# A four-layer Perceiver kernel: short steps of both passes together, queries at steps 4 to 6, the row constants at step 47, keys' and values' weights as two loads, and two more pieces in one feed-forward

## The chip, the cores and the metric

The kernel runs on one core of a Trainium2 chip, in one launch. The metric is the device time in microseconds (us). A core has five engines with instruction streams of their own: TensorE (PE, with PEld for its weight loads), VectorE (DVE), ScalarE (ACT), GpSimd (POOL) and SyncE (SP). SP and POOL issue nearly all transfers here, each in the order of its own queue; 16 DMA engines carry them.

## The reference

128 query rows x (128 x 256) pass through four layers. Each layer has a cross-attention over a context of 12,544 rows of 256, then an attention or mixing block on the 128 rows, then a feed-forward block. Everything is float32, with 16 heads of 16. The cross-attentions are what the change touches most:

```python
q = _split_heads(hidden_states @ q_w.T + q_b)
k = _split_heads(context @ k_w.T + k_b)
v = _split_heads(context @ v_w.T + v_b)
scores = jnp.einsum('bhqd,bhkd->bhqk', q, k) / jnp.sqrt(jnp.float32(HD))
scores = jnp.where(mask, -jnp.inf, scores)
probs = jax.nn.softmax(scores, axis=-1)
ctx = jnp.einsum('bhqk,bhkd->bhqd', probs, v)
```

Layer 1 adds a 128 x 12,544 table (`fside`) to the scores of every head, layers 0 and 3 mask some of the keys, and layers 1 to 3 project the result (`O @ Wo + bo`). The feed-forward of layer 1 is a mixture of 8 experts (`h = x @ w1 + b1`, layer norm, gelu, `@ w2 + b2`, the two best gates); that of layer 2 is a piecewise-linear gelu on numbers rounded to multiples of 2^-8, with 33 breakpoints.

## The kernel before

Twelve blocks run one after another: l0x, l0a, l0f, l1x, l1a, l1f, l2x, l2a, l2f, l3x, l3a, l3f (x: cross-attention, a: attention, f: feed-forward).

**Cross-attention (`cross`, from L419).** The 16 heads are taken as 4 units of 4 heads. The array of TensorE is used as four row tiles of 32, one for each head of a unit. The 12,544 keys are taken in 25 steps (`NST`) of 512 (`ST`); the last step of a unit has only 256 keys, and is called the short step here. Each unit passes over the keys twice:

- Pass 1, `score_s` (L498 on): scores with the queries on the partitions (matmul L515, tile `_s`). VectorE takes the maximum of each head's bank (L528; in l1x L523, which adds `fside` too). After a unit's last step `raised` puts the negative maximum into `low` (L538), and `lower` (L546, L547) adds it to the unit's queries, so that pass 2 yields scores less their maximum.
- Pass 2, `score_t` (L554 on): the scores transposed, keys on the partitions (L573, tile `_t`); ScalarE takes the exponential (L590, or L580 for two heads at once); in l1x VectorE adds the transposed `fside` first (L585). `values` multiplies by the values (L634, tile `_p`) and adds into `acc` (L640). `finish` transposes and divides (L645 to L650).

Pass 2 runs `lead` = 27 steps behind pass 1. Step `at` makes pass 1 of step `km = at` and pass 2 of step `ke = at - 27`, counted over all units from 0 to 99. So steps 0 to 26 hold pass 1 alone, steps 27 to 99 are mixed, steps 100 to 126 hold pass 2 alone. In a mixed step `scores` (L599) makes two sets: scores of heads 2, 3 beside transposed scores of heads 0, 1, and then the other way round. The matmuls of a set run on different row tiles at the same time. Short steps are number 24 of each unit: pass 1 takes them at 24, 49, 74 and 99, pass 2 at 51, 76, 101 and 126. In pass 2 alone, outside l1x, PSUM is taken as pairs of banks (`alone`, `pairs`), one exponential covers two heads, and `values` takes two steps at once.

**Order by hand.** The whole loop of `cross` stands under `manual_schedule`: each engine runs its instructions as the code issues them. So do the tail of l3x and all of l3a. In the other blocks a scheduler orders the instructions by their costs.

**Pieces.** Keys and values of all four layers are projected from the context by small jobs, the pieces, in one long list (`self.jobs`). A key piece is a projection of 128 columns for 512 keys (two matmuls 128x512, L373, tile `_k`); a value piece is one of 256 keys (four matmuls 128x256, tile `_v`). `pump(n)` runs the next n of them. In `cross` a goal and a `rate` say how many a step takes. In the other blocks `one`, which hands out a PSUM bank, adds `share` to a credit and pumps a piece for each whole one; l1f sets `share` to 0.9 (L1061). In l2f `pump(1)` stands behind every second breakpoint but the last (L1231).

A visit is 512 keys of one layer and one part ("k" or "v"). `load` (L185) fetches its context (tile `_c`) on SP's queue, three visits ahead. Results go to DRAM on POOL's queue (`kx` L220, `vx` L246) and come back on SP's: key tiles `kt` of 1,024 keys (`keys`, mask row L290 and four heads L294, 17 tiles held) and value tiles `vt` (`values`, L307, three tiles). `fetch_k(at + 2)` and `fetch_v` at the head of a step ask for what is used two steps later.

**Loads at the start.** SP's queue carries x, `l0x_kvw` (128 x 1024, the weights of keys and values, L194), the context of visit 0 (c0) and of visit 1 (c1), the columns of constants `cols` (L201), `cst` (L202), and visit 2. POOL's queue carries `w_l0x`, the weights of the queries (`ahead`, L323; `weight` asks for it). At step 2 of l0x POOL issues `rows`, a broadcast of 2,940 floats to 128 partitions (L663), and `ahead(2)` fetches the weights `w_l0a`; the next one, for l0f, follows.

**Queries.** `query(g)` (L450 on) makes the queries of unit g: two matmuls with the transposed normed x, and VectorE's scaling (L461). Unit 0 is made before the loop, units 1 to 3 at steps 12, 37 and 62.

## Time and profile before

Three runs took 2293.19, 2289.47 and 2293.31 us, median 2293.19. The profiled execution took 2290.23 us, its span is 2288.4 us, at a mean granted TensorE clock of 0.99. By stretches of the span (the blocks' bounds are rounded):

| stretch, us | blocks | PE busy | DVE busy | ACT busy | granted clock |
|---|---|---|---|---|---|
| 0 to 145 | l0x, steps 0 to 24 | 134.0 | 66.9 | 36.5 | 0.98 |
| 145 to 460 | l0x, the rest | 313.2 | 233.8 | 159.3 | 1.00 |
| 460 to 590 | l0a, l0f | 123.9 | 30.5 | 73.7 | 1.00 |
| 590 to 1210 | l1x | 615.9 | 514.9 | 322.1 | 0.99 |
| 1210 to 1405 | l1a, l1f | 193.5 | 98.8 | 97.4 | 1.00 |
| 1405 to 1760 | l2x | 349.4 | 266.4 | 214.5 | 1.00 |
| 1760 to 1835 | l2a, l2f | 69.3 | 45.1 | 36.5 | 0.98 |
| 1835 to 2190 | l3x | 347.5 | 266.7 | 211.1 | 1.00 |
| 2190 to 2288 | l3a, l3f | 86.0 | 27.1 | 25.4 | 0.93 |

The busy time of an engine is the time in which it had at least one instruction at work. PE counts as busy at half clock too, and also when only one of its row tiles has work. A clock of 1.00 is full speed. Groups and timelines name an instruction by its line, its output and its inputs, with how often it ran (x4) and the time; for TensorE the records count double, since a float32 matmul is recorded as two. Waits read "engine tile line <- what released it: total us, times, longest us".

### The profile page before, as it was taken

The page shows a single profiled execution, that of the slowest core. Times are in us where ns is not written, and L with a number is a line of the kernel's source. Part 1 is how long each engine was busy: PE and PEld are TensorE (multiplying, and loading weights), DVE is VectorE, ACT ScalarE, POOL GpSimd, SP SyncE. Part 2 cuts the span into 40 slices and gives each one's busy share as a digit, 9 for nine tenths or more (in the row PEclk, how much of TensorE's full clock was granted, in tenths as well). Part 3 has the DMA queues.
Part 4 walks back from the last instruction along what each step waited for, and adds up shares of the span by engine and source line. Part 5 has one row for each costly group of instructions (what it writes and reads, how often), then busy time and mean ns, then how long its engine had stood idle before and what let it go on. Part 6 is the DMA issues. An engine that isn't in the chain of part 4 may idle for free.

```text
span 2288.4 us, 76016 instructions
## 1 busy us (share of the span) xinstructions
PE 2232.8 (98%) x32141; PEld 1682.5 (74%) x32141; DVE 1550.2 (68%) x3391; ACT 1176.5 (51%) x2020; POOL 326.7 (14%) x587
## 2 busy tenths in 40 slices
PE   8999999999999999999999999999999999999979
PEld 3368888875647887666778854588888867888868
DVE  3476688713187789999987545988861699888231
ACT  2213366674323555555684364266677515666832
POOL 4331100002241110101001123200000440000001
PEclk9999999999999999999999999999999999999989
DMA  8886633228898887888766688633332863333217
GB/s 303 261 258 202 220 108 93 75 73 299 297 304 271 276 256 229 251 243 255 228 203 212 220 314 271 177 89 99 90 86 83 277 200 105 89 89 95 60 44 242
DMA packets 220977, 431.86 MB, mean 189 GB/s; under 512 B 31236, under 2 KB 87576, under 8 KB 216544
## 3 DMA queue, kind: packets, MB, share of 16 engines
q1 hardware_dynamic: 181440, 270.87, 40.7%
q0 software_dynamic: 38976, 156.03, 19.1%
q8 instruction: 256, 4.19, 0.8%
q14 instruction: 81, 0.66, 0.1%
q10 hardware_dynamic: 224, 0.10, 0.0%
HBM read 320.72 MB, written 106.16 MB: 187 GB/s over the span
## 4 chain that ended last, share of the span: by engine, by line
PE 54%; DVE 3%; ACT 2%; DMA 1%; issue 1%; POOL 1%; POOLq 0%; ACTq 0%; DVEq 0%
PE l3x_t L573 5%; PE l2x_t L573 5%; PE l2x_p L634 4%; PE l3x_p L634 4%; PE l2x_k L373 4%; PE l1x_t L573 4%; PE l3x_k L373 4%; PE l3x_s L515 3%; PE l1x_p L634 3%; PE l2x_s L515 3%; PE l2x_v L373 3%; PE l3x_v L373 2%; PE l1x_s L515 2%; PE l3f_h L373 1%; PE l3f_o L373 1%
## 5 line engine op out<-in xcount | busy, mean ns | idle before, releaser
L590 ACT ACTIVATE l1x_e<-l1x_e 128x512 f32<-128x512 f32 (+1 forms) x400 | 240.6, 622 | 209.1 <-DVE l1x_e L585 209.1
L528 DVE TENSOR_REDUCE l0x_mxs<-l0x_s 128x1 f32<-128x512 f32 (+1 forms) x400 | 244.3, 672 | 98.8 <-PE l0x_s L515 66.9
L523 DVE CUSTOM_DVE_ANT_0 l1x_j<-l1x_s,l1x_f 128x512 f32<-128x512 f32 (+1 forms) x400 | 252.9, 675 | 41.4 <-PE l1x_t L573 23.6
L528 DVE TENSOR_REDUCE l3x_mxs<-l3x_s 128x1 f32<-128x512 f32 (+1 forms) x400 | 242.4, 671 | 30.1 <-PE l3x_t L573 24.7
L528 DVE TENSOR_REDUCE l2x_mxs<-l2x_s 128x1 f32<-128x512 f32 (+1 forms) x400 | 242.3, 671 | 29.5 <-PE l2x_t L573 24.7
L585 DVE TENSOR_TENSOR l1x_e<-l1x_t,l1x_g 128x512 f32<-128x512 f32 (+1 forms) x400 | 250.0, 672 | 10.9 <-PE l1x_t L573 9.0
L590 ACT ACTIVATE l0x_e<-l0x_t 128x512 f32<-128x512 f32 x292 | 149.5, 596 | 167.4 <-PE l0x_t L573 164.4
L573 PE MATMUL l1x_t<-l1x_qb,kt 32*128 32x128 f32 x3136 | 203.0, 285 | 0.9 <-DVE l1x_e L585 0.7
L515 PE MATMUL l1x_s<-kt,l1x_qb 32*128 32x512 f32 (+1 forms) x800 | 196.2, 630 | 1.0 <-DMA kt<-l1x_kx 0.7
L590 ACT ACTIVATE l3x_e<-l3x_t 128x512 f32<-128x512 f32 x292 | 149.7, 595 | 82.0 <-PE l3x_t L573 78.9
L515 PE MATMUL l3x_s<-kt,l3x_qb 32*128 32x512 f32 (+1 forms) x800 | 188.2, 617 | 0.0
L590 ACT ACTIVATE l2x_e<-l2x_t 128x512 f32<-128x512 f32 x292 | 149.7, 595 | 74.7 <-PE l2x_t L573 71.6
L515 PE MATMUL l2x_s<-kt,l2x_qb 32*128 32x512 f32 (+1 forms) x800 | 187.2, 610 | 0.0
L515 PE MATMUL l0x_s<-kt,l0x_qb 32*128 32x512 f32 (+1 forms) x800 | 181.9, 614 | 2.0 <-DMA kt<-l0x_kx 2.0
L573 PE MATMUL l3x_t<-l3x_qb,kt 32*128 32x128 f32 x3136 | 179.0, 279 | 1.4 <-ACT l3x_e L580 0.8
L573 PEld LDWEIGHTS l1x_t<-l1x_qb,kt 32*128 32x128 f32 x3136 | 171.1, 188 | 11.6 <-DVE l1x_e L585 4.7
L573 PE MATMUL l2x_t<-l2x_qb,kt 32*128 32x128 f32 x3136 | 178.1, 278 | 1.5 <-ACT l2x_e L580 0.8
L573 PE MATMUL l0x_t<-l0x_qb,kt 32*128 32x128 f32 x3136 | 177.0, 278 | 1.4 <-ACT l0x_e L580 0.8
L573 PEld LDWEIGHTS l3x_t<-l3x_qb,kt 32*128 32x128 f32 x3136 | 159.9, 187 | 6.2 <-ACT l3x_e L580 3.7
L573 PEld LDWEIGHTS l2x_t<-l2x_qb,kt 32*128 32x128 f32 x3136 | 159.4, 186 | 6.7 <-ACT l2x_e L580 3.7
L573 PEld LDWEIGHTS l0x_t<-l0x_qb,kt 32*128 32x128 f32 x3136 | 158.5, 186 | 5.8 <-ACT l0x_e L580 3.7
L634 PE MATMUL l1x_p<-l1x_e,vt 128*32 128x128 f32 x3136 | 113.2, 279 | 2.1 <-ACT l1x_e L590 1.9
(602 smaller groups left out, 3773.4 us busy)
## 6 DMA issues: line engine op xcount, KB each, us to landing
l1x_f<-in_fside SPq DMA_DIRECT2D x96, 256.0 KB
l1x_g<-in_fsideT SPq DMA_DIRECT2D x96, 256.0 KB
w<-in_w_l3f POOLq DMA_DIRECT2D x16, 1024.0 KB, 5.1
l0x_vx<-l0x_vs POOLq DMA_DIRECT2D x24, 544.0 KB, 5.4
vt<-l0x_vx SPq DMA_DIRECT2D x48, 272.0 KB
l1x_vx<-l1x_vs POOLq DMA_DIRECT2D x24, 544.0 KB, 5.9
vt<-l1x_vx SPq DMA_DIRECT2D x48, 272.0 KB
l2x_vx<-l2x_vs POOLq DMA_DIRECT2D x24, 544.0 KB, 4.4
```

What stands on the lines that cost most here:

```text
L373: self.nc.tensor.matmul(out, a, b, start=(i == 0), stop=(i == len(lhs) - 1))
L515: nc.tensor.matmul(banks[j][:, :m], qb[u][r, :], t[r, at : at + m], start=True, stop=True)
L523: nc.vector.tensor_tensor_reduce(out=junk[:, :m], in0=banks[j][:, :m], in1=ft[k][:, :m], scale=1.0, scalar=-3.0e38, op0=ALU.add, op1=ALU.m ...
L528: nc.vector.tensor_reduce(out=mxs[u][:, j, i : i + 1], in_=banks[j][:, :m], axis=AX.X, op=ALU.max)
L573: nc.tensor.matmul(banks[j][:, a * P : (a + 1) * P], t[r, at + a * P : at + (a + 1) * P], qb[u][r, :], start=True, stop=True)
L585: nc.vector.tensor_tensor(out=e[:, j, :m], in0=src, in1=gt[k][:, : m // P, :].rearrange("p a q -> p (a q)"), op=ALU.add)
L590: nc.scalar.activation(e[:, j, :m], src, AF.Exp)
L634: nc.tensor.matmul(ps[32 * c : 32 * c + 32, :P], lhs, rhs, start=n < 4, stop=n >= len(todo) - 4, skip_group_check=True)
```

## The change

- `load` fetches the weights as two tiles, `kw` before the first key visit and `vw` before the first value visit of a layer. `cols` moves ahead of c1; `w_l0x` is issued on SP's queue behind `cst`, instead of on POOL's.
- `rows` and the weights behind it are issued at step 47 of l0x instead of step 2.
- `placed` reorders pass 2 within a unit: the short step is taken at position 22, and steps 22 and 23 come behind it. So the short steps of both passes fall into the same mixed step (49, 74, 99). The value tile is picked by the number of tiles fetched so far, and the pairs of pass 2 alone follow the new order.
- Queries 1 to 3 are made at the first steps from 4 on that take a piece, instead of steps 12, 37, 62.
- `finish` of units 0 and 1 moves from steps 54 and 79 to steps 75 and 100.
- l1f's `share` is 0.82 instead of 0.9; l2f pumps two pieces behind its last breakpoint, where it pumped none.

```diff
@@ -189,17 +189,20 @@
             return
         name, part, s, m = self.visits[at]
         nc = self.nc
-        if part == "k" and s == 0:
-            w = self.bp.tile([P, 1024], F32, name=f"{name}_kvw", tag="kvw", bufs=2)
-            nc.sync.dma_start(out=w, in_=self.io[f"w_{name}_kv"])
-            self.kvw[name] = w
+        if s == 0:
+            w = self.bp.tile([P, 512], F32, name=f"{name}_{part}w", tag=f"{part}w", bufs=2)
+            half = slice(0, 512) if part == "k" else slice(512, 1024)
+            nc.sync.dma_start(out=w, in_=self.io[f"w_{name}_kv"][:, half])
+            self.kvw[name, part] = w
         c = self.bp.tile([P, 2, ST], F32, name=f"{name}_c{part}{s}", tag="ctx", bufs=4)
         nc.sync.dma_start(out=c[:, :, :m],
                           in_=self.io["ctxT"][:, s : s + m].rearrange("(c p) k -> p c k", p=P))
         self.ctx[at] = c
+        if at == 0:
+            nc.sync.dma_start(out=self.cols, in_=self.io["cols"])
         if at == 1:
-            nc.sync.dma_start(out=self.cols, in_=self.io["cols"])
             nc.sync.dma_start(out=self.cst, in_=self.io["cst"])
+            self.ahead(1)
 
     def project(self, at, name, part, b, s, m, last):
 
@@ -210,7 +213,7 @@
         def keys(half):
             if half == 0:
                 self.load(at + 3)
-            wk = self.kvw[name][:, 0:512].rearrange("p (c f) -> p c f", c=2)
+            wk = self.kvw[name, "k"].rearrange("p (c f) -> p c f", c=2)
             k = self.bp.tile([P, ST], F32, name=f"{name}_ks{b}_{s}_{half}", tag="kst", bufs=4)
             ps = self.bank(f"{name}_k{b}_{s}_{half}")
             self.mm(ps[:, :m], [wk[:, c, half * P : (half + 1) * P] for c in range(2)],
@@ -224,7 +227,7 @@
                 self.load(at + 3)
             wd = WIDTH[name]
             u = 16 // wd
-            wv = self.kvw[name][:, 512:1024].rearrange("p (c f) -> p c f", c=2)
+            wv = self.kvw[name, "v"].rearrange("p (c f) -> p c f", c=2)
             if a == 0:
                 t["v"] = self.bp.tile([P, u, 4, 17 * wd], F32, name=f"{name}_vs{b}_{s}", tag="vst",
                                       bufs=3)
@@ -303,7 +306,7 @@
             return
         n = min(SB, S2 - s) // P * 68
         self.until(name, b, "v")
-        v = self.vts[(NSB * (4 * CROSS.index(name) + u) + b) % 3]
+        v = self.vts[len(self.vt) % 3]
         self.nc.sync.dma_start(out=v[:, :n],
                                in_=self.vx[name, b][u].rearrange("p a e -> p (a e)"))
         self.vt[name, u, b] = v
@@ -311,7 +314,7 @@
 
 
     def weight(self, key):
-        self.ahead(self.plan.index(key) + (3 if self.loaded else 1))
+        self.ahead(self.plan.index(key) + (3 if self.loaded > 1 else 1))
         return self.tiles.pop(key)
 
     def ahead(self, n):
@@ -320,7 +323,8 @@
             name, i = self.plan[self.loaded]
             src = self.io[name] if i is None else self.io[name][i]
             t = self.wp.tile([P, WT], F32, name=f"w{self.loaded}", tag="w")
-            self.nc.gpsimd.dma_start(out=t[:, : src.shape[1]], in_=src)
+            queue = self.nc.gpsimd if self.loaded else self.nc.sync
+            queue.dma_start(out=t[:, : src.shape[1]], in_=src)
             self.tiles[self.plan[self.loaded]] = t
             self.loaded += 1
 
@@ -482,9 +486,10 @@
                     nc.sync.dma_start(out=f[:, :m], in_=self.io["fside"][:, s : s + m])
                     ft[k] = f
 
-            def fetch_v(k):
-                if not 0 <= k < units * NST:
+            def fetch_v(p):
+                if not 0 <= p < units * NST:
                     return
+                k = placed(p)
                 self.values(name, k)
                 if side:
                     s, m = k % NST * ST, min(ST, S2 - k % NST * ST)
@@ -493,6 +498,12 @@
                         out=f[:, : m // P, :],
                         in_=self.io["fsideT"][s : s + m, :].rearrange("(a p) q -> p a q", p=P))
                     gt[k] = f
+
+            def placed(p):
+
+
+                u, i = divmod(p, NST)
+                return u * NST + (i if i < NST - 3 else NST - 1 if i == NST - 3 else i - 1)
 
             def tile_of(u, j):
 
@@ -547,16 +558,12 @@
                 nc.vector.tensor_tensor(out=qb[u][r, :], in0=qb[u][r, :], in1=ps[r, :P],
                                         op=ALU.add)
 
-            def alone(k):
-
-                return not side and k >= total - lead
-
             def score_t(k, heads):
 
                 u, i = divmod(k, NST)
                 s, m = i * ST, min(ST, S2 - i * ST)
                 t, at = kt[name, u, s // SB], s % SB
-                if alone(k):
+                if pairs:
                     twos = [self.two(f"{name}_t{k}_{j}") for j in (0, 2)]
                     banks = {j: twos[j // 2][:, j % 2, :] for j in heads}
                 else:
@@ -575,7 +582,7 @@
                                              start=True, stop=True)
 
                 def drain():
-                    if alone(k):
+                    if pairs:
                         for j in (0, 2):
                             nc.scalar.activation(e[:, j : j + 2, :m], twos[j // 2][:, :, :m], AF.Exp)
                         return
@@ -652,14 +659,14 @@
                                         in1=den.unsqueeze(2).to_broadcast([P, width, 16]),
                                         op=ALU.mult)
 
-            due, waiting, pairs = 0.0, [], False
+            due, waiting, pairs, asked = 0.0, [], False, 1
             n_k = 2 * NST
             n_own = n_k + S2 // 256
             with tc.manual_schedule():
                 for k in (0, 1):
                     fetch_k(k)
                 for at in range(total + lead + 3):
-                    if first and at == 2:
+                    if first and at == lead + 20:
                         nc.gpsimd.dma_start(out=self.rows,
                                             in_=self.io["rows"].to_broadcast([P, NROW]))
                         self.ahead(2)
@@ -669,7 +676,8 @@
                         pairs = True
                     fetch_k(at + 2)
                     fetch_v(at + (1 if pairs else 2) - lead)
-                    ke = at - lead if 0 <= at - lead < total else None
+                    pe = at - lead if 0 <= at - lead < total else None
+                    ke = None if pe is None else placed(pe)
                     km = at if at < total else None
 
 
@@ -685,26 +693,31 @@
                     due -= more
                     inner = 1 if side and mixed and pieces == 1 else 0
                     scores(ke, km, lambda: self.pump(inner))
-                    if at < total - NST and at % NST == 12:
-                        query(at // NST + 1)
+
+
+                    if asked < 4 and at >= 4 and (pieces or at >= NST - 4):
+                        query(asked)
+                        asked += 1
                     if 0 < at <= total and at % NST == 0:
                         lower(at // NST - 1)
+                        if at >= 3 * NST:
+                            finish(at // NST - 3)
                     self.pump(pieces - inner)
 
 
                     while waiting:
-                        n = 2 if pairs and (waiting[0] + 1) % NST and waiting[0] + 1 < total else 1
+                        n = 2 if pairs and waiting[0] % NST != NST - 3 else 1
                         last = waiting[0] + n - 1
-                        if ke is not None and ke - last < (2 if pairs else 1):
+                        if pe is not None and pe - last < (2 if pairs else 1):
                             break
                         if last > waiting[-1]:
                             break
-                        values(waiting[:n])
+                        values([placed(p) for p in waiting[:n]])
                         waiting = waiting[n:]
-                    if ke is not None:
-                        waiting.append(ke)
+                    if pe is not None:
+                        waiting.append(pe)
                     u, i = divmod(at - lead - 2 - NST, NST)
-                    if i == 0 and 0 <= u < units:
+                    if i == 0 and 2 <= u < units:
                         finish(u)
             if pairs:
                 self.banks("one")
@@ -1058,7 +1071,7 @@
     def l1_ffn(self):
 
         nc = self.nc
-        self.side, self.share = False, 0.9
+        self.side, self.share = False, 0.82
         E = 8
         with self.tc.tile_pool(name="l1f", bufs=1) as pool, \
                 self.tc.tile_pool(name="l1f_h", bufs=2) as hp:
@@ -1228,8 +1241,8 @@
                                             op0=ALU.is_gt)
                     nc.gpsimd.tensor_scalar(out=h, in0=h, scalar1=0.0, scalar2=None, op0=ALU.max)
                     nc.gpsimd.tensor_tensor(out=far, in0=far, in1=h, op=ALU.mult)
-                if i % 2 and i < 14:
-                    self.pump(1)
+                if i % 2:
+                    self.pump(1 if i < 14 else 2)
             nc.vector.tensor_tensor(out=y, in0=y, in1=near, op=ALU.mult)
             nc.vector.tensor_tensor(out=y, in0=y, in1=far, op=ALU.add)
             self.fixed(y, y)
```

## The prediction

> **What bounds the kernel now.** I read the engines' shares first, then the chain of waits.
>
> ```profile
> span 2288.4 us, 76016 instructions
> PE 2232.8 (98%) x32141; PEld 1682.5 (74%) x32141; DVE 1550.2 (68%) x3391; ACT 1176.5 (51%) x2020; POOL 326.7 (14%) x587
> PE 54%; DVE 3%; ACT 2%; DMA 1%; issue 1%; POOL 1%; POOLq 0%; ACTq 0%; DVEq 0%
> ```
>
> TensorE is busy for 98% of the span and idle for only 2288.4 − 2232.8 = 55.6 us. So filling holes can bring little; the rest must come from TensorE time that is wasted while "busy": row tiles at which only one of two passes works, and half clock. Next TensorE's waits, and SP's:
>
> ```profile
> PE l0x_k L373 <- DMA l0x_ck<-in_ctxT: 8.9, 1, 8.9
> PE l2f_o L373 <- DVE l2f_y L1181: 4.5, 1, 4.5
> PE l0x_s L515 <- DMA kt<-l0x_kx: 2.0, 1, 2.0
> ...
> SPq L294 <- DMA l0x_kx<-l0x_ks: 29.6, 12, 12.2
> ```
>
> The 8.9 is the start, the 2.0 lies at 58 us, and SP's longest wait (12.2) runs up to it. The windows there, with TensorE first and the granted clock in the third place from the right:
>
> ```profile
> 50.00:55.00 5.00, 5.00 (x18) 1.81 (x18) 2.78 (x6) 0.00 (x0) 1.00 (x2) 1.00 1.02 395
> 55.00:60.00 5.00, 2.95 (x11) 1.36 (x10) 1.12 (x2) 2.56 (x4) 1.92 (x4) 1.00 0.73 264
> 60.00:65.00 5.00, 5.00 (x10) 1.79 (x8) 2.58 (x4) 0.00 (x0) 1.80 (x3) 0.52 0.95 311
> 65.00:70.00 5.00, 5.00 (x16) 1.75 (x15) 0.47 (x1) 1.38 (x2) 1.05 (x2) 0.80 0.92 281
> ```
>
> 2.05 us are idle, and then TensorE runs at half clock (0.52) for 6.83 us (from 60.22 to 67.05 in the clock's own record).
>
> **1. The start.** The first matmul waits for c0 (8.91), which shares the DMA engines with x, 512 KB of weights and, on POOL's queue, w_l0x. They land at x 3.15, weights 5.05, w 8.46, c0 8.78. Ahead of c0 there are then x 0.13, weights 0.26 and c0 0.52 MB, and nothing on POOL's queue. Before, 1.95 MB (0.13 + 0.52 + 0.78 + 0.52) were through at 8.8; at the 382 to 411 GB/s of the first 50 us, 1.04 MB less (0.26 and w's 0.78) is 2.5 to 2.7 us less. I take −2.9, the landing at about 6.0, since the first loads start slowly and cols is out of c1's way. Bounds: −0.5 (c0's 1.9 us of issue and flight after the weights stays as it is) and −3.2. What hides the rest: w and cst land at about 11, just ahead of the first query matmul, which was at 14.39. From the first k to the first score it is one chain, so all that follows moves along.
>
> **2. rows, away from step 2.** rows (1.5 MB) and two weights (0.77 MB each) go into POOL's queue at 39.98 to 42.5. The kx writes behind them land at 54.9 to 57.3 instead of 3.8 us after issue, so SP's kt read stands until 56.74:
>
> ```profile
> 39.80 3.77 SPq L197 DMA_DIRECT2D l0x_ck<-in_ctxT  x2
> 43.98 0.50 SPq L290 DMA_DIRECT2D kt<-mask_row  x1
> 56.74 1.71 SPq L294 DMA_DIRECT2D kt<-l0x_kx  x4
> ```
>
> On VectorE the steps' starts are 48.94, 53.64, 60.47, 69.53, 74.23, so 4.70 undisturbed, then 6.83 and 9.06: 2.13 + 4.36 = 6.5 us lost. I take −6.5 (bounds: −4, if pieces' own traffic stalls a step anyway, and −6.7).
>
> The Trainium skill ("TensorE: Matmul & The Clock Gate", "HAM oscillation — how this bites in real kernels") says that TensorE loses its clock only in idle gaps of over about 3.4 us. The rows differ: a gap of 2.05 us preceded 6.83 us at 0.52. By the rule alone the part would be worth the 2.1 of the wait, and the sum 4.4 less.
>
> **3. rows, at step 47.** The same 3.05 MB now start near 284 (before's times) and need 3.05 MB / 400 GB/s = 7.6 us, to 292. In POOL's queue only the values' write of 281.30 stands before them. On SP the last value tile, then unit 2's first key tile (5 DMAs) stand in this stretch:
>
> ```profile
> 283.75 2.01 SPq L294 DMA_DIRECT2D kt<-l0x_kx  x4
> 287.27 0.34 SPq L307 DMA_DIRECT2D vt<-l0x_vx  x1
> 289.25 0.50 SPq L290 DMA_DIRECT2D kt<-mask_row  x1
> ```
>
> The key tile is issued by 291.6 and used by the score at 292.95, which comes 0.9 earlier after part 4. Steps here are 3 us, so the two steps of prefetch are 6 us, against 9.4 at step 2. I take +1: bounds 0 (landing in time) and +5 (a wait of 1.6, and one 3.41 us stretch at half clock twice over).
>
> The skill ("DMA: Bandwidth & Descriptors", "Queues, rings and completion order") says that each DMA engine takes packets from its queues in turn, which speaks against this move: SP's reads would run at half rate. No row shows it at this place; by it the key tile lands 2.5 us late, and the sum is 1.5 worse.
>
> **4. Short steps together** (steps 49, 74, 99). A mixed step makes both passes on separate row tiles, so a set lasts as long as the longer one. Short scores beside a full t:
>
> ```profile
> 289.94 0.48 PE L515 MATMUL l0x_s<-kt,l0x_qb 32*128 32x256 f32 x2
> ...
> 290.28 0.95 PE L573 MATMUL l0x_t<-l0x_qb,kt 32*128 32x128 f32 x14
> ...
> 291.94 1.08 PE L634 MATMUL l0x_p<-l0x_e,vt 128*32 128x128 f32 x32
> ```
>
> The two sets last 289.94 to 291.94, that is 2.0, like a full step's (287.0 to 288.9); two steps later a short t lies beside full scores, 2.0 again. Together the short halves need two sets of 0.55 (half of 1.0, plus some fill), so 1.1 + 2.0 against 4.0: −0.92 per pairing, values' matmuls unchanged. VectorE isn't in the way: four half reductions and an addition are 1.24 + 0.28 = 1.5, against 1.1 + 1.0 of TensorE. Three pairings: −2.76. In pass 2 alone step 101 is full instead of short, +0.45 (t is 2.07 per two steps); the block's last step is full, so its last two exponentials (0.94 each instead of half) stand open: +0.5. So −1.8 per block, −5.4 for l0x, l2x and l3x (bounds −1.0 and −2.6 each, −3 and −7.8).
>
> In l1x VectorE sets the pace: per step four L523 and four L585 at 0.675 and 0.672 (0.63 undisturbed) are 5.05, of the 5.03 to 5.3 that a step takes. Pairing moves VectorE's work and removes none: 0, bounds ±1.5. finish(0) and finish(1), moved to steps 75 and 100, are the same instructions: 0.
>
> **5. Queries beside pieces.** A query is four matmul records and one VectorE pass of 0.34. At step 12 of l2x VectorE's reductions start 1584.77 and 1588.39, 3.62 apart against 3.05: 0.55, and as much at two more steps. At steps 4 to 6 there is a VectorE-bound step of 2.4 with pieces; there it costs about 0.4 each. −0.5 in l2x and l3x, −0.3 in l0x, +0.1 in l1x: −1.2 (bounds −0.2 and −2).
>
> **6. Pieces.** l1f gets four k matmuls fewer (68 for 72, each 0.86, two records): −3.4, since TensorE is busy there for 154.73 of 155 us. They come back as eight v matmuls in l2f (two records of 0.23 each; 0.43 from start to start): 3.4. The 4.47 us that l2f_o waits could hide them, but by the changed order all eight stand behind l2f_o; there they fill only the 0.42 us before l3x_xnT: +2.9. Sum −0.5 (−3.5, if they get into the wait; +3, if l1f is left idle).
>
> **Sum.** −2.9 − 6.5 + 1 − 5.4 + 0 − 1.2 − 0.5 = −15.5, from the profiled execution's 2290.2 (span 2288.4): 2274.7. The median of the runs, 2293.2, is 3.0 above that, the lowest 2289.5 below it. I put the forecast between 2274.7 and 2277.7: 2276.
>
> **Rivals.** (a) The pairings bring nothing, because VectorE or the last exponentials set the pace: −15.5 + 5.4 = −10.1, so 2280 to 2283. For: in l2x four reductions fill 2.48 of 3.05 us. Against: TensorE has no idle time in these steps. 13%. (b) The moved rows collide at step 50 as they did at 58: a wait of 5 and two slow stretches, 3.4, more: −15.5 + 7.5 = −8, so 2282 to 2285. For: the key tile comes 1 us ahead of use even now. Against: only one write in POOL's queue, and no piece. 10%. (c) Slower: at the unit boundaries the paired steps leave TensorE idle for the wait on VectorE's maximum (0.78 before l3x_mr), and its clock halves, as at 1900 us (window 0.66). One stretch of 3.41 us costs 1.7, two cost 3.4; it decides from 15.5 / 12 = 1.3 us per boundary. With 12 boundaries and two stretches +41 − 15.5 = +25: 2315 to 2318; with one, +5: 2295 to 2298. Against: l0x and l2x show no half clock at the same place. 6%. (d) The pieces and short steps do not do what they should: the wait before l2f_o stays, as the order says (in the forecast). If it is filled after all, −3 more: 2273. 3%.
>
> **How the numbers follow.** The forecast has 68%. Its parts' bounds, taken as independent (the root of the squared distances), are about 4 below and 7 above 2276; with 3 us between executions it runs from 2267 to 2283. (a) and (b) reach 2285, so the range is 2267 to 2285, which leaves out (c) and the tails. A measurement of this kernel can't tell 0.2%, 4.6 us, from no change. Faster: forecast, (d), (a) and most of (b): 0.88. Same: the rest of (b), of the bounds and the mild (c): 0.07. Slower: 0.05.
>
> **What would show it.** First matmul at about 6; no half clock at 60 and steps of 4.7 throughout 40 to 75; paired steps of 2.1 us at 49, 74 and 99 and no lost clock at the boundaries; the score of step 50 at most 1 us late; l2f_o's wait still 4.5. It is wrong if the half clock only moves (to step 50, or the boundaries), or if VectorE's steps stay at 3.05 where the short ones are paired.

## The result, and the profile after

The changed kernel takes 2295.74 us (median of 20 runs, 2292.13 to 2303.85), the kernel before 2291.66 us (20 runs, 2285.44 to 2297.72). The ratio is 1.0021, with a 95% interval of 1.0012 to 1.0029. It is slower by 4.1 us, where 15.5 us of gain were forecast. The profiled execution took 2295.71 us.

The engines' shares and TensorE's longest waits in the changed kernel (lines have moved: L526 is the score, L580 the transposed score, L377 a projection, L362 a transposition):

```profile
span 2293.9 us, 76014 instructions
...
PE 2232.3 (97%) x32141; PEld 1684.2 (73%) x32141; DVE 1550.4 (68%) x3391; ACT 1179.2 (51%) x2022; POOL 326.3 (14%) x586
```

```profile
PE l0x_k L377 <- DMA l0x_ck<-in_ctxT: 7.8, 1, 7.8
PE l0x_s L526 <- DMA kt<-l0x_kx: 4.8, 1, 4.8
PE l2f_o L377 <- DVE l2f_y L1194: 4.0, 1, 4.0
...
PE l1f_xnT_ps L362 <- DVE l1f_xn L350: 2.3, 1, 2.3
```

TensorE's busy time is as before (2232.8), and its idle time grew from 55.6 to 61.6. The wait at the start fell by 1.1. The wait on a key tile, 2.0 before, is 4.8; a wait of 2.3 is new. Where the time went can be read from the first and last matmul of each block in both profiles (worked out from their starts and ends):

| up to | after minus before, us | change in the stretch |
|---|---|---|
| first score of l0x | −1.4 | −1.4 |
| l0x, end of step 48 | −7.6 | −6.2 |
| l0x, last value | −2.1 | +5.5 |
| l1x's norm (l0a, l0f) | −1.6 | +0.4 |
| l1f's norm (l1x, l1a) | −3.5 | −1.9 |
| l1f's last output | +1.1 | +4.6 |
| l2x, last value | −0.3 | −1.4 |
| first score of l3x (l2a, l2f) | +3.3 | +3.6 |
| l3x, last value | +2.8 | −0.5 |
| end (l3a, l3f) | +5.6 | +2.7 |

So the start and step 2 gave what looks like the forecast, and three places took it back: l0x behind step 48, l1f, and l2f. The last stretch has no change in its code. In the seventeen executions traced in this study it lasted 100.9 to 106.9 us (101.8 in the kernel before's profile, 104.5 in the changed one's), so its 2.7 us can be chance.

**The stall has moved.** The windows of the changed kernel around step 49 (TensorE, weight loads, VectorE, ScalarE, POOL; then granted clock, DMA share, GB/s):

```profile
280.00:285.00 5.00, 5.00 (x123) 4.19 (x116) 4.53 (x12) 3.38 (x8) 0.00 (x0) 1.00 1.00 365
285.00:290.00 5.00, 0.20 (x2) 0.48 (x4) 0.35 (x2) 0.00 (x0) 0.00 (x0) 0.72 1.01 294
290.00:295.00 5.00, 5.00 (x61) 4.41 (x63) 2.47 (x4) 2.08 (x4) 0.00 (x0) 0.60 0.59 148
```

TensorE stands for 4.8 us, from 285.0 to 289.8, and from 287.20 on its clock is at half for 6.83 us. The picture that the kernel before shows at 40 to 67 us is here again. The timelines of POOL and of SP show why:

```profile
273.72 0.75 POOL L249 DMA_DIRECT2D l0x_vx<-l0x_vs  x1 [3.98 <-DVE l0x_vs L246]
274.46 0.55 POOL L670 DMA_DIRECT2D rows<-in_rows  x1
275.01 0.55 POOL L327 DMA_DIRECT2D w<-in_w_l0a  x1
275.55 1.05 POOL L327 DMA_DIRECT2D w<-in_w_l0f  x2
```

```profile
278.00 0.34 SPq L310 DMA_DIRECT2D vt<-l0x_vx  x1
278.44 0.50 SPq L293 DMA_DIRECT2D kt<-mask_row  x1
278.99 1.83 SPq L297 DMA_DIRECT2D kt<-l0x_kx  x4
280.98 0.34 SPq L310 DMA_DIRECT2D vt<-l0x_vx  x1
281.67 0.50 SPq L293 DMA_DIRECT2D kt<-mask_row  x1
286.99 2.10 SPq L297 DMA_DIRECT2D kt<-l0x_kx  x4
```

rows is issued at 274.46, 0.74 us behind the last value write and in the same queue, with three weights behind it, not two: 3.8 MB. Behind it SP asks for the unit's last value tile (68 KB, at 278.00), and from 278.44 on for the first key tile of unit 2, which step 50 needs. The trace also has the transfers' packets: those of rows run from 276.52 to 282.92; the value tile's begin at 281.75, the key tile's at 283.85. The key tile's four heads land between 288.02 and 289.86, 9.0 to 9.5 us after their issue, and TensorE goes on at 289.80. In the kernel before, the value tile's packets began 0.97 us after its issue (287.27), and the key tile, asked for from 283.19 on, had its packets from 284.66 to 287.42.

So the key tile was asked for in time and landed late. SP itself stands from 282.17 to 286.99, until the value tile has landed (4.8 us in SP's waits), but that holds up only the next key tile, on which step 52 did not wait. Steps 49 to 51 last 7.44, 5.04 and 3.27 us; the same steps of the next unit, 74 to 76, last 2.46, 3.34 and 3.32. That is 15.75 against 9.12, a loss of 6.6 us.

**l1f.** TensorE at the passage from l1a to l1f, before and after:

```profile
1327.39 1.03 PE L373 MATMUL l1a_pr<-w,l1a_ooT 128*128 128x256 f32 x4
1328.25 2.74 PE L373 MATMUL l3x_k<-l3x_ck,l3x_kvw 128*128 128x512 f32 x6
1330.83 0.38 PE L358 MATMUL l1f_xnT_ps<-cst,l1f_xn 128*128 128x128 f32 x2
...
1332.27 1.96 PE L373 MATMUL l1f_h<-w,l1f_xnT 128*128 128x512 f32 x4
```

```profile
1324.05 1.03 PE L377 MATMUL l1a_pr<-w,l1a_ooT 128*128 128x256 f32 x4
1327.34 0.41 PE L362 MATMUL l1f_xnT_ps<-cst,l1f_xn 128*128 128x128 f32 x2 [2.26 <-DVE l1f_xn L350]
1328.27 1.02 PE L377 MATMUL l1f_g<-cols,l1f_xnT 128*128 128x8 f32 x4 [0.52 <-DVE l1f_xnT L364]
1329.14 3.76 PE L377 MATMUL l1f_h<-w,l1f_xnT 128*128 128x512 f32 x4
```

The three key matmuls (six records) that covered the norm are gone. TensorE waits 2.26 and 0.52 us, and behind that the same four records of l1f_h take 3.76 instead of 1.96: half clock, 6.83 us from 1328.26 in the clock's record.

### The profile page after: what moved, and what is told of

It is laid out like the page before. It is cut to its first block, busy times and chain, and to the rows that moved or that the text cites. A ratio compares the mean times of both kernels' runs of the same rounds, so it can differ in the third digit from the quotient of the medians.

```text
span 2293.9 us, 76014 instructions
## 1 busy us (share of the span) xinstructions
PE 2232.3 (97%) x32141; PEld 1684.2 (73%) x32141; DVE 1550.4 (68%) x3391; ACT 1179.2 (51%) x2022; POOL 326.3 (14%) x586
## 4 chain that ended last, share of the span: by engine, by line
PE 57%; ACT 3%; DVE 2%; issue 0%; DMA 0%; DVEq 0%; ACTq 0%; POOLq 0%
PE l3x_t L580 5%; PE l2x_t L580 5%; PE l3x_p L641 4%; PE l2x_p L641 4%; PE l2x_k L377 4%; PE l1x_t L580 4%; PE l2x_v L377 4%; PE l3x_s L526 4%; PE l3x_k L377 4%; PE l2x_s L526 3%; PE l1x_p L641 3%; PE l3x_v L377 3%; PE l1x_s L526 2%; PE l3f_h L377 1%; PE l3f_o L377 1%; DVE l2x_mxs L539 1%
## 5 line engine op out<-in xcount | busy, mean ns | idle before, releaser
L539 DVE TENSOR_REDUCE l3x_mxs<-l3x_s 128x1 f32<-128x512 f32 (+1 forms) x400 | 242.4, 671 | 30.2 <-PE l3x_t L580 24.7
L539 DVE TENSOR_REDUCE l2x_mxs<-l2x_s 128x1 f32<-128x512 f32 (+1 forms) x400 | 242.4, 671 | 26.9 <-PE l2x_t L580 24.7
L597 ACT ACTIVATE l0x_e<-l0x_t 128x512 f32<-128x512 f32 (+1 forms) x292 | 148.6, 593 | 170.9 <-PE l0x_t L580 170.1
L580 PE MATMUL l1x_t<-l1x_qb,kt 32*128 32x128 f32 x3136 | 201.8, 284 | 0.5
L526 PE MATMUL l1x_s<-kt,l1x_qb 32*128 32x512 f32 (+1 forms) x800 | 195.6, 628 | 1.2 <-DMA kt<-l1x_kx 1.2
L597 ACT ACTIVATE l3x_e<-l3x_t 128x512 f32<-128x512 f32 (+1 forms) x292 | 148.6, 592 | 79.4 <-PE l3x_t L580 79.3
L526 PE MATMUL l3x_s<-kt,l3x_qb 32*128 32x512 f32 (+1 forms) x800 | 189.2, 620 | 0.0
L526 PE MATMUL l2x_s<-kt,l2x_qb 32*128 32x512 f32 (+1 forms) x800 | 186.3, 610 | 0.5 <-DVE l2x_qb L465 0.5
L526 PE MATMUL l0x_s<-kt,l0x_qb 32*128 32x512 f32 (+1 forms) x800 | 181.6, 617 | 4.8 <-DMA kt<-l0x_kx 4.8
L597 ACT ACTIVATE l2x_e<-l2x_t 128x512 f32<-128x512 f32 (+1 forms) x292 | 148.6, 592 | 71.7 <-PE l2x_t L580 71.6
L580 PE MATMUL l3x_t<-l3x_qb,kt 32*128 32x128 f32 x3136 | 178.5, 279 | 2.2 <-ACT l3x_e L587 1.5
L580 PE MATMUL l0x_t<-l0x_qb,kt 32*128 32x128 f32 x3136 | 177.9, 280 | 2.2 <-ACT l0x_e L587 1.5
L580 PE MATMUL l2x_t<-l2x_qb,kt 32*128 32x128 f32 x3136 | 177.7, 279 | 2.2 <-ACT l2x_e L587 1.5
L580 PEld LDWEIGHTS l1x_t<-l1x_qb,kt 32*128 32x128 f32 x3136 | 169.4, 187 | 12.4 <-DVE l1x_e L592 5.7
L580 PEld LDWEIGHTS l3x_t<-l3x_qb,kt 32*128 32x128 f32 x3136 | 159.6, 187 | 7.2 <-ACT l3x_e L587 4.5
L580 PEld LDWEIGHTS l0x_t<-l0x_qb,kt 32*128 32x128 f32 x3136 | 159.6, 187 | 6.1 <-ACT l0x_e L587 4.5
L580 PEld LDWEIGHTS l2x_t<-l2x_qb,kt 32*128 32x128 f32 x3136 | 158.8, 186 | 7.0 <-ACT l2x_e L587 4.5
```

The costliest lines, as they stand in the source:

```text
L526: nc.tensor.matmul(banks[j][:, :m], qb[u][r, :], t[r, at : at + m], start=True, stop=True)
L539: nc.vector.tensor_reduce(out=mxs[u][:, j, i : i + 1], in_=banks[j][:, :m], axis=AX.X, op=ALU.max)
L580: nc.tensor.matmul(banks[j][:, a * P : (a + 1) * P], t[r, at + a * P : at + (a + 1) * P], qb[u][r, :], start=True, stop=True)
L597: nc.scalar.activation(e[:, j, :m], src, AF.Exp)
```

## The experiments

Times of one kernel differ by 10 us and more between executions, so single runs are read by the steps and stretches of their traces, not by their totals. A step's length is the time from its first score matmul to the next step's. "Old" and "new" mean as in the kernel before and as changed.

**1. rows at step 102.** Edit to the changed kernel:

```diff
-                    if first and at == lead + 20:
+                    if first and at == total + 2:
```

> The changed kernel with one edit: rows and the weights behind them are issued at step 102 of l0x, where pass 2 runs alone, instead of step 47. In the changed kernel step 49 lasts 7.44 us and step 50 5.04 us; the same pair at steps 74 and 75 lasts 2.46 and 3.34. Theory A (the four transfers of POOL's queue, 3.8 MB, hold up unit 2's first key tile): steps 49 and 50 fall to about 2.46 and 3.1 to 3.4, no half clock follows, the block l0x ends 6.0 to 6.7 us earlier, total about 2289 us. Rival B (the paired short steps themselves, with the maximum at the unit's boundary, stall TensorE there): steps 49 and 50 stay near 7.4 and 5.0. Rival C (the collision moves along): a wait of TensorE on a transfer of over 1 us appears between steps 102 and the end of l0a, and the total stays near 2295.

Steps 49 to 51 took 7.36, 5.55 and 3.20; TensorE waited 4.7 us on the key tile. Read alone, this fits rival B. POOL's timeline says otherwise:

```profile
275.08 0.75 POOL L249 DMA_DIRECT2D l0x_vx<-l0x_vs  x1 [3.98 <-DVE l0x_vs L246]
275.82 0.55 POOL L670 DMA_DIRECT2D rows<-in_rows  x1
```

The step number had moved by 55, the transfer not at all. In POOL's instructions of l0x nothing stands between the last value write and rows, and rows waits for nothing. An engine with nothing to wait for runs ahead of the loop. "At step 47" meant "right behind the last value write", and so would any later step.

**2. rows held back.** POOL first copies one column of a running sum that VectorE writes at that step:

```diff
-                    if first and at == lead + 20:
+                    if first and at == total + 2:
+                        nc.gpsimd.tensor_copy(self.rows[:, 0:1], acc[2][:, 0:1])
```

> The changed kernel, but rows and the weights behind them are held back until step 102 by a small copy on POOL that reads the running sum of unit 2 (before it in POOL's queue). Moved in the code alone to step 102, they were still issued at 276 us, at once behind POOL's last value write, and steps 49 and 50 still took 7.4 and 5.6 us. Theory A (POOL, which waits for nothing there, runs ahead of the steps; it is its transfers that hold up unit 2's first key tile): rows is now issued after 430 us, step 49 takes about 2.46 and step 50 3.1 to 3.4, TensorE's wait of 4.4 to 4.8 us on the key tile is gone, l0x's mixed steps last 6 to 7 us less than the 292 of the other runs. Rival B (SP's own queue, the value tile behind the last value write, holds the key tile up without any help of POOL): the wait stays over 3 us though rows is issued after 430.

```profile
443.49 0.18 POOL L670 COPY rows<-l0x_at 128x1 f32<-128x1 f32 x1 [167.89 <-DVE l0x_at L647]
443.97 0.55 POOL L671 DMA_DIRECT2D rows<-in_rows  x1 [0.30 <-POOL rows L670]
```

The copy held POOL for 167.89 us. Steps 49 to 51 took 2.57, 3.07 and 3.58, together 9.22 instead of 15.75: theory A holds, the transfers were the cause, and 6.5 us is their price here. But the stretch from the last score to the last value grew from 62.49 to 67.67 us. Two windows there (same columns):

```profile
450.00:455.00 5.00, 4.35 (x135) 3.84 (x135) 0.29 (x1) 2.55 (x3) 0.00 (x0) 1.00 0.99 392
455.00:460.00 5.00, 3.73 (x115) 3.15 (x108) 0.29 (x1) 3.77 (x4) 0.00 (x0) 1.00 0.74 271
```

The DMA share is 0.99 at 450 to 455, TensorE has holes (4.35 and 3.73 us busy of 5), and half clock follows (3.41 us from 462.92). Pass 2 alone reads value tiles all the time. Rows and weights in one lump (3.0 MB at step 2, 3.8 later) cost 5.2 to 6.6 us at each of the three places tried.

**3. Queries at their old steps.**

```diff
-                    if asked < 4 and at >= 4 and (pieces or at >= NST - 4):
-                        query(asked)
-                        asked += 1
+                    if at < total - NST and at % NST == 12:
+                        query(at // NST + 1)
```

> The changed kernel with the queries of units 1 to 3 back at steps 12, 37 and 62, all else as changed. Theory A (the early queries free the buffer of l0x's weights, so that a fourth transfer, a second expert weight of l0f, joins rows at step 47): only one l0f weight is issued at step 47, and the wait of TensorE on the key tile before unit 2's first score falls from 4.8 us to 2 to 3.5 us. Rival B: the wait is set by rows alone and stays at 4.5 to 5. For the queries themselves: every block's first phase is 1.3 us shorter and steps 12, 37 and 62 cost 0.45 to 0.65 more each, so 0.3 to 1.0 us per cross block against it; together 2 us of loss without the gain at step 47.

Only one weight of l0f was issued at once: the early queries do free the buffer. Yet the wait was 4.4 us, and steps 49 to 51 took 7.08, 5.80 and 3.03, 15.91 in all. The fourth transfer costs nothing; rows and what lies just behind it suffice, near rival B. For the queries: in l2x the first 28 steps were 1.12 us shorter, and steps 37 and 62 0.64 longer each. Early queries bring 0.16 us there.

**4. Old pieces.** l1f's share 0.9, no pieces behind l2f's last breakpoint.

```diff
-        self.side, self.share = False, 0.82
+        self.side, self.share = False, 0.9
...
-                if i % 2:
-                    self.pump(1 if i < 14 else 2)
+                if i % 2 and i < 14:
+                    self.pump(1)
```

> The changed kernel with l1f's share back at 0.9 and l2f without the two added pieces. In the changed kernel l1f ends 4.5 us later, against its own start, than before, though it has four key matmuls fewer, and the first score of l3x stands 3.6 us later against the end of l2x. Theory A (the smaller share took the three key matmuls that stood between l1a's projection and l1f's transposed norm, TensorE waits 2.3 us there and runs at half clock after): this wait is gone, no half clock near 1328, l1a and l1f together last 3 to 5 us less than in the changed kernel; l2f to l3x's first score 3 to 3.6 us less; total 2287 to 2290. Rival B (only a half-clock stretch by chance, not the share): the same wait of over 1.5 us before l1f's transposed norm stays, and l1f gains nothing.

```profile
1323.51 1.03 PE L377 MATMUL l1a_pr<-w,l1a_ooT 128*128 128x256 f32 x4
1324.38 2.74 PE L377 MATMUL l3x_k<-l3x_ck,l3x_kw 128*128 128x512 f32 x6
1326.95 0.38 PE L362 MATMUL l1f_xnT_ps<-cst,l1f_xn 128*128 128x128 f32 x2
```

The three key matmuls are back, the wait and the half clock gone. From l1f's norm to its last output it takes 70.14 us, exactly as before, against 74.76. From l2f_o's end to the first score of l3x it takes 7.25, as before, against 10.10. Theory A, with 4.6 and 2.9 us.

The eleven executions with the share of 0.82 show what the 4.6 is made of. All have the two waits. Seven have 6.83 us at half clock behind them and take 74.5 to 74.8; three have 3.41 and take 73.4 to 73.8; one (run 8) has none and takes 72.05. All six with 0.9 take 70.14 or 70.15. So the smaller share costs 1.9 us without the half clock and up to 4.6 with it, 4.0 in the mean.

The 2.9 us of l2f do not show in this run's total alone: the wait before l2f_o was 6.67 us here (4.01 in the changed kernel), so from l2f_h's end to l3x's first score only 1.3 of them are left. Run 15 has the same pieces and 6.53; why it was longer in these two was not tested.

**5. finish at its old steps.** finish of units 0 and 1 back at 54 and 79.

```diff
-                        if at >= 3 * NST:
-                            finish(at // NST - 3)
...
-                    if i == 0 and 2 <= u < units:
+                    if i == 0 and 0 <= u < units:
```

> The changed kernel with finish of units 0 and 1 back at steps 54 and 79. In the changed kernel pass 2 alone begins with waits of TensorE on ScalarE of 0.62 and 0.42 us (0.31 and 0.20 before), and the stretch from step 99 to the last values is 1.2 to 1.5 us longer than before in l0x, l2x and l3x, against 0.0 predicted. Theory A (finish at step 100 takes a two-bank PSUM tile, on top of lower's, that the next transposed scores need): from step 100 to the block's end 0.7 to 1.0 us less, while step 79 is 0.3 to 0.4 longer; net -0.3 to -0.7 per block. Rival B (the extra time is all at the block's end, where the last step is full): the stretch from step 100 stays as long, and step 79 takes 0.35 more: +0.3 per block.

In l2x the stretch from step 99 to the last value fell from 64.15 to 63.24 (−0.9): theory A's first half. At steps 54 and 55 a finish costs 0.59, more than expected; at the unit's boundary (75) it costs nothing, since steps 75 and 76 sum to 6.66 with and without it. So moving it brings about 0.3 us per block, where theory A's net was a loss of 0.3 to 0.7. And it splits what looked like the gain of a pairing: of the 0.87 us that steps 49 to 56 gained against before, 0.59 was finish and 0.28 the pairing.

**6. Old order of pass 2 in all units**, and **7. in the last unit alone.**

```diff
-                return u * NST + (i if i < NST - 3 else NST - 1 if i == NST - 3 else i - 1)
+                return p
...
-                        n = 2 if pairs and waiting[0] % NST != NST - 3 else 1
+                        n = 2 if pairs and (waiting[0] + 1) % NST and waiting[0] + 1 < total else 1
```

> The changed kernel with pass 2 in its old order (short step last in each unit), all else as changed, finish of units 0 and 1 at steps 75 and 100 too. With finish at its old steps, the five steps from 49 took 15.2 us in the changed order against 15.4 before, and the two steps that held finish 0.6 more, so that of the 0.87 us that a pairing seemed to bring 0.28 would be the pairing and 0.59 finish. Theory A (that split is right, and the block's end pays for the order): steps 49 to 53 take 15.4 in l2x and l3x, the mixed steps 0.5 to 0.7 us more in all than in the changed kernel, and the stretch from step 99's end 0.8 to 1.3 us less, so that the block is 0.2 to 0.8 us faster without the pairing. Rival B (pairing is worth the predicted 0.92): the mixed steps take 1.8 us more, and the block is slower by 0.5 or more.

```diff
                 u, i = divmod(p, NST)
+                if u == units - 1:
+                    return p
```

> The changed kernel with the old order in the last unit alone, so that each block ends on a short step, as before. Theory A (the full last step leaves its last two exponentials and more values open at the block's end): the stretch from step 99's end to the last value 0.4 to 0.6 us less in l0x, l2x and l3x, and in l1x, where VectorE adds the table first, 0.8 to 1.5 less. Rival B (the end is paid at its beginning, at step 100): under 0.2 us less.

Old order everywhere: in l2x the mixed steps were 0.74 us longer (0.24 around step 49, 0.50 around 74) and the stretch from step 99 0.80 shorter, 63.35. So the pairing as a whole costs 0.06 us per block: between the theories, and next to A (0.2 to 0.8). In l0x, where the transfers still lie behind the last value write, steps 49 to 53 took 20.40 in this run, against 15.49 in the kernel before: without the pairing the collision costs 4.9 instead of 6.6. Old order in the last unit: the stretch from the last score to the last value fell by 0.69, 0.69 and 0.70 us in l0x, l2x and l3x, and by 2.60 in l1x (there 1.3 us of it are value pieces that go back into l1a). That is theory A, and more than expected. The end of l2x before and as changed (TensorE), and ScalarE as changed:

```profile
1756.49 0.73 PE L573 MATMUL l2x_t<-l2x_qb,kt 32*128 32x128 f32 x16
1757.35 2.39 PE L634 MATMUL l2x_p<-l2x_e,vt 128*32 128x128 f32 x80
```

```profile
1755.14 1.17 PE L580 MATMUL l2x_t<-l2x_qb,kt 32*128 32x128 f32 x32
1756.25 1.72 PE L641 MATMUL l2x_p<-l2x_e,vt 128*32 128x128 f32 x52
1758.40 1.07 PE L641 MATMUL l2x_p<-l2x_e,vt 128*32 128x128 f32 x28 [0.43 <-ACT l2x_e L587]
```

```profile
1756.41 1.94 ACT L587 ACTIVATE l2x_e<-l2x_t 128x1024 f32<-128x1024 f32 x2 [1.05 <-PE l2x_t L580]
```

The last transposed product has 32 records instead of 16 and two exponentials of 0.97 behind it; the last values wait for the second.

**8. The boundary's VectorE work one step later**, and **9, 10. left out altogether**, in both orders. The first edit moves `raised` and `lower`, the second removes both calls:

```diff
-                if km is not None:
-                    raised(km)
...
-                    if 0 < at <= total and at % NST == 0:
+                    if 0 < at <= total:
+                        raised(at - 1)
+                    if 1 < at <= total + 1 and at % NST == 1:
                         lower(at // NST - 1)
```

> The changed kernel with VectorE's closing maximum of a unit and its negation, and the addition to the queries that hangs on them, one step later (after steps 50, 75 and 100 instead of 49, 74 and 99; pass 2 first needs them at 52). In the changed kernel steps 49 to 53 of l2x last 2.46, 3.08, 3.58, 2.97 and 3.08, sum 15.17, against 15.44 before. Theory A (VectorE sets the pace here: with 0.43 us of closing maximum and 0.28 of addition on top of the reductions it frees the score banks of step 50 late, and TensorE gives back at step 51 what the paired step saved): step 51 falls to 3.0 to 3.1, the five steps to 14.5 to 14.8 in l2x and l3x. Rival B (TensorE's own order, the transposed product at the boundary and the queries' lowering, makes step 51 long): step 51 or 52 stays at 3.5, the sum at 15.1 to 15.3.

> The changed kernel without the work at the units' boundaries: the closing maximum, its negation, and the matmul and addition that lower the queries are left out, so scores are not reduced by their maximum. Pass 2 in the changed order. To be read beside the next run, which has the old order. Theory A (the boundary's VectorE work takes the gain of the pairing): steps 49 to 53 in l2x fall from 15.17 to 14.0 to 14.4, and lie 0.8 or more under the old order's. Rival B (VectorE's reductions alone, four of 512 columns per step and an addition, hold TensorE to 15 us whatever the order): 14.5 to 15.0, and the old order within 0.4 of it.

> The same without boundary work, pass 2 in the old order. Theory A: steps 49 to 53 in l2x 15.0 to 15.2, 0.8 or more over the changed order's. Rival B: within 0.4 of it.

Steps of l2x, in us:

| kernel | 49 | 50 | 51 | 52 | 53 | sum |
|---|---|---|---|---|---|---|
| before | 2.95 | 3.51 | 2.92 | 2.70 | 3.36 | 15.44 |
| changed | 2.46 | 3.08 | 3.58 | 2.97 | 3.08 | 15.17 |
| one step later | 2.46 | 2.54 | 4.30 | 3.04 | 3.02 | 15.36 |
| left out, new order | 2.46 | 2.54 | 3.52 | 2.97 | 3.08 | 14.57 |
| left out, old order | 2.90 | 2.98 | 2.92 | 2.70 | 3.35 | 14.85 |

Moving that work later brought nothing: theory A of run 8 fell, and step 51, at 4.30, went past rival B's 3.5 too. Leaving it out shortened both orders by 0.6, and the new order is still only 0.28 ahead: rival B of runs 9 and 10. The paired step gets shorter, 2.46 instead of 2.95 (the forecast had 2.1), but step 51 gives most of it back, 3.5 instead of 2.9. VectorE there, in the run without boundary work:

```profile
1543.81 2.48 DVE L539 TENSOR_REDUCE l2x_mxs<-l2x_s 128x1 f32<-128x512 f32 x4 [0.73 <-PE l2x_t L580]
1546.21 0.28 DVE L645 TENSOR_TENSOR l2x_at<-l2x_at,l2x_p 128x128 f32<-128x128 f32 x1
1546.41 2.48 DVE L539 TENSOR_REDUCE l2x_mxs<-l2x_s 128x1 f32<-128x512 f32 x4
1548.85 0.29 DVE L645 TENSOR_TENSOR l2x_at<-l2x_at,l2x_p 128x128 f32<-128x128 f32 x1
1549.87 2.48 DVE L539 TENSOR_REDUCE l2x_mxs<-l2x_s 128x1 f32<-128x512 f32 x4 [0.73 <-PE l2x_t L580]
```

From 1543.81 to 1549.14 (5.3 us, steps 50 and 51) VectorE has no hole, and TensorE's weight loads wait on its reductions there (1.1 us in all from 1543 to 1556). It needs 2.7 us per full step and TensorE 3.0; when TensorE gains half a microsecond on it, VectorE is the one that is late. That is read from this timeline; no run made VectorE's reductions shorter.

**11. Four value pieces ahead of l2f_o.** l2f in an order written by hand, with l1f's share back at 0.9 and no pieces behind the last breakpoint.

```diff
+            with self.tc.manual_schedule():
...
+                self.pump(4)
                 ps = self.one("l2f_o")
```

> The changed kernel with l1f's share back at 0.9, and l2f in an order written by hand with four pieces ahead of l2f_o, 79 value matmuls between l2f_h and l2f_o instead of 68. Theory A (value matmuls that stand ahead of l2f_o hide the 4.0 to 4.5 us that it waits for l2f_y): the wait falls under 1 us, no half clock follows it near 1825, and from l2f_h's end to l3x's first score it takes 2 to 4 us less than the changed kernel's 49.8, about 46 to 48, with the eight matmuls of the two pieces inside. Rival B (pieces ahead of l2f_o delay l2f_y itself, through ScalarE's copies): l2f_o starts later than 33.4 us after l2f_h's end, and the wait stays over 2.

```profile
1831.61 5.84 PE L377 MATMUL l3x_v<-l3x_vw,l3x_cv 128*128 128x256 f32 x14 [3.69 <-ACT l3x_vs L244]
1838.06 3.72 PE L377 MATMUL l2f_o<-w,l2f_y 128*128 128x256 f32 x16 [0.60 <-DVE l2f_y L1194]
```

The wait before l2f_o fell to 0.60, but l2f_o came 41.2 us behind l2f_h instead of 33.4: TensorE now waits 3.69 for ScalarE's copy of the values, with 6.83 us at half clock from 1829.99, and from l2f_h's end to l3x's first score it takes 54.6 instead of 49.8. That is rival B's later start; the long wait has moved ahead of the value matmuls. Whether the pieces or the order by hand did it was not separated.

**12. The old start.** The changed kernel with one load of 512 KB, cols behind c1, w_l0x on POOL.

```diff
-            queue = self.nc.gpsimd if self.loaded else self.nc.sync
-            queue.dma_start(out=t[:, : src.shape[1]], in_=src)
+            self.nc.gpsimd.dma_start(out=t[:, : src.shape[1]], in_=src)
```

> The changed kernel with the old start: keys' and values' weights as one load of 512 KB, cols behind the second context tile, the queries' weights on POOL's queue. Ten executions with the new start had the first matmul at 6.95 to 7.97 us and the first score at 23.8 to 25.4 (mean 24.6); two with the old one 8.9 and 8.3, and 25.2 and 25.4. Theory A (the new start is worth about 1 us at the first matmul, and only 0.7 at the first score, since the way from the first matmul to the score grows from 16.3 to 17): first matmul 8.2 to 9.0, first score 25.2 to 25.6. Rival B (worth nothing; the executions differ that much by themselves): first score at 24.7 or earlier.

First matmul at 9.38, first score at 26.24. Over all executions of this study the first matmul stands at 8.25 to 9.38 with the old start (three) and 6.95 to 8.05 with the new one (fourteen), and the first score at 25.6 against 24.7 in the mean. Run 12 itself lies a little beyond theory A's ranges, and the means are near it, with 1.0 us; the scores of the two groups overlap (25.2 to 26.2, and 23.8 to 25.4).

**13. rows and weights one by one, on the kernel before**, at steps 55, 59, 63, 68 and 73, each held back on POOL; **14, 15. the same with the changed kernel's better parts.**

```diff
-                    if first and at == 2:
-                        nc.gpsimd.dma_start(out=self.rows,
+                    if first and at in (55, 59, 63, 68, 73):
+                        nc.gpsimd.tensor_copy(o[:, D - 1 : D], acc[(at - lead - 2) // NST][:, 0:1])
...
+                            part = slice(0, 1470) if at == 55 else slice(1470, NROW)
...
+                            self.ahead(2 + (at - 63) // 5)
```

> The kernel before with one edit: rows in two halves and three weights one by one at steps 55, 59, 63, 68 and 73 of l0x, held back on POOL by a small copy, instead of all at step 2. Theory A (the loss at step 2 was 6.5 us and is not paid again): no half clock near 60 us, first phase's steps all 4.70, no wait of TensorE on a transfer from step 50 to 80; 2291.7 - 6.5 = 2285, 0.997. Rival B (the loss comes back where the transfers now lie): 0.999 to 1.001. This trace also gives the old start a second time: first matmul 8.9 and first score 25.2 if the start is the same in every execution.

> The changed kernel with: pass 2 reordered in units 0 and 1 alone; finish of unit 1 back at step 79 (unit 0's stays at 75); the old pieces in l1f and l2f; and rows in two halves and three weights, one by one at steps 55, 59, 63, 68 and 73, each held back by a small copy on POOL that reads the running sum of that step. Against the changed kernel: no wait on a key tile at step 50 (-6.5), l1f -4.5 and l2f to l3x -2.9 as with the old pieces, the blocks' ends -0.7 each in l0x, l2x, l3x and -2.6 in l1x. Theory A (these costs are separate and the transfers of 0.75 MB fit between two key tiles): -6.5 - 4.5 - 2.9 - 2.1 - 2.6 = -18.6, so 2277 us, 0.994 of the kernel before. Rival B (each 0.75 MB still holds a key tile up, by 1 to 2 us): 2280 to 2287, with waits of TensorE on a key tile between 300 and 380 us. Rival C (half-clock stretches come back elsewhere): 2285 to 2292.

> The changed kernel with: pass 2 reordered in units 0 and 1 alone, its pairs of steps cut at the unit's end in units 2 and 3; finish of unit 1 back at step 79; the old pieces in l1f and l2f; rows in two halves and three weights one by one at steps 55, 59, 63, 68 and 73, held back on POOL. The version before it, in which one pair of steps in unit 2 read a value tile too late, gained 7.0 us to the end of l0x's mixed steps and spent 2282 us, against 2288.4 for the kernel before in its profile, and 0.9985 of it in twelve runs. Theory A (the separate gains hold: 7 in l0x, 1.5 to 2 in each later cross block): 2278 to 2285, 0.995 to 0.998 of the kernel before. Rival C (half-clock stretches take it back): 0.999 to 1.001.

Run 13: in its trace no clock is lost near 60 us, the two steps that had taken 6.83 and 9.08 take 4.70, and the steps 49 to 99 are as before to 0.01 us. l0x ends 5.6 us earlier. In twelve runs it took 0.9988 of the kernel before (0.9974 to 1.0002), an interval that ends just short of theory A's 0.997 and reaches into rival B's 0.999 to 1.001. POOL in run 15:

```profile
302.92 0.18 POOL L672 COPY l0x_o<-l0x_at 128x1 f32<-128x1 f32 x1 [27.06 <-DVE l0x_at L649]
303.05 0.55 POOL L675 DMA_DIRECT2D rows<-in_rows  x1
315.10 0.18 POOL L672 COPY l0x_o<-l0x_at 128x1 f32<-128x1 f32 x1 [11.50 <-DVE l0x_at L649]
```

Each transfer of 0.75 MB waits for its step, and no score of l0x waits on a key tile. Run 14 took 0.9985 (0.9970 to 1.0000); in one pair of steps of unit 2 it multiplies with a value tile that has been overwritten. Run 15 cuts that pair: 2283.73 us in twelve runs against 2290.11 of the kernel before, a ratio of 0.9972 (0.9957 to 0.9987). It is faster than the kernel before, and by the two ratios than the changed one, beside which it did not run. That is theory A of run 15 (0.995 to 0.998), and a smaller gain than the 0.994 expected of run 14. The gain in l0x came as expected (it ends 7.0 us earlier); half clock takes part of it back in some executions: run 15's profile, 2294.0 us, has 52 us at half clock, run 14's, 2283.8, has 36.

## Why the prediction was wrong, step by step

The steps that failed are 3 (rows at step 47), 4 (the price of a pairing) and l1f in 6. Of eight terms one, l1f's, had the wrong sign; with it four were mis-sized by 1.9 us and more, all four to the same side. Forecast −15.5; the measured terms below sum to −1.0 − 6.5 + 6.6 − 0.9 − 0.5 − 1.2 + 4.6 + 2.9 = +4.0, against +4.1 between the medians. That close a match is luck: most terms come from single traces, and the two profiles differ by 5.6 us. The forecast also held that 0.2% can't be told from no change here; twenty runs of each told 0.21% (0.12 to 0.29).

- **1, the start: forecast −2.9, measured −1.0.** Inside the bounds, by two wrong readings. The sum took w_l0x at 0.78 MB; the DMA view has 512 KB (0.52 MB), so at its own rate the saving was 2 us. And c0 landed near 7.8, not 6.0. The step took for granted that a queue's transfers finish in turn, so that only what stands ahead of c0 counts. The packets rule it out: cols stands behind c0 in SP's queue, yet by 7.0 us 0.35 MB of cols had moved, while the last packets of c0 ended at 7.05 at the earliest.
- **2, rows away from step 2: forecast −6.5, measured −6.5.** Steps 5 and 6 of the changed kernel, less their queries, are 4.70 each. The mechanism (kx writes behind rows, SP standing, half clock) was right. The trace was also right against the page. The Trainium skill ("TensorE: Matmul & The Clock Gate", "HAM oscillation — how this bites in real kernels") puts the limit at gaps of about 3.4 us, while gaps of 2.05 (the kernel before, step 5) and 2.26 us (l1f, the changed kernel's profile) were each followed by 6.83 us at half clock.
- **3, rows at step 47: forecast +1, bound +5, measured +6.6.** The risk was the right one, the key tile's landing, but its cost was wrong. The forecast let two steps, 6 us, cover a tile whose landing it left nearly as it was, and its bound allowed a wait of 1.6. In place of that the tile, asked for behind rows, landed 9.0 to 9.5 us after its issue, and TensorE stood for 4.8 us and lost clock. Run 2 shows that the transfers are the cause. That POOL runs ahead (run 1) adds little here: rows was issued 1.9 us before step 47 began (276.31). Nor does the third weight matter (run 3). Rival (b) named this collision at 10%, at +7.5 on top of +1. The row in the prediction that should have raised it is SP's 12.2 us of standing at step 2, which was read as a matter of the kx writes in POOL's own queue alone. The Trainium skill ("DMA: Bandwidth & Descriptors", "Queues, rings and completion order") has each DMA engine take packets from its queues in turn, which spoke against the move; the estimate by it was a key tile 2.5 us late. The run showed more: with a value tile asked for at 278.00, SP's queue moved its first packet at 281.75, when most of rows had gone.
- **4, pairings: forecast −1.8 per block, measured about −0.3** (−0.12 in l2x, −0.40 in l3x, −0.39 in l0x, of which finish's move is some −0.3). Two prices were off. "−0.92 per pairing" counted TensorE's sets alone; VectorE, called "not in the way" for the paired step, is in the way in the next two, so 0.24 to 0.5 is left. And the block's end, forecast at +0.45 and +0.5 less a third pairing (0.03 in sum), cost 0.8 us net: 0.69 for the full last step (run 7), and 0.1 for the third pairing and the full step 101 together, forecast at −0.47 (runs 6 and 7). finish, forecast at nothing, gained 0.59 twice and cost 0.7 to 0.9 at step 100, where PSUM is taken in pairs of banks. Rival (a), at 13%, was this. That VectorE holds the steps behind the paired one is read from its timeline; the 0.24 to 0.5 is measured.
- **l1x: forecast 0, measured about −0.5.** Its end is 2.75 us longer, and l1a behind it 3.2 shorter. Its steps ahead of the end are 1.3 shorter, 0.3 of it the queries'; this profile has 3.4 us less at half clock in l1x than the one before, so how much of the rest is the change's stays open.
- **5, queries: forecast −1.2, measured about −1.2:** −0.28 in l0x, −0.31 in l1x, −0.16 in l2x, −0.43 in l3x.
- **6, pieces, l1f: forecast −3.4, measured +4.6** in the profile, 4.0 in the mean of eleven executions: the largest miss, and no rival named it. "TensorE is busy there for 154.73 of 155 us" is why four matmuls less looked like a gain. They were what kept it busy: the smaller share took them from the one place where nothing else covers a norm. The forecast had the changed order of instructions to read, and read only the counts in it; it shows nothing between l1a_pr and l1f_xnT_ps. **l2f: forecast +2.9, measured +2.9,** read from the same order.

Rival (c), the half clock at every paired step, did not come. Besides the stall at l0x's step 50, one stretch of 3.41 us begins at a paired step (l1x, 853.81); the kernel before had two there (855.52 and 865.76).
